# Two tiles at a time: the q/k/v projections of an attention pass by seven block products instead of eight

## The chip, the cores and the metric

The kernel runs on one core of a Trainium2 chip, all in float32. A core has five engines, each with its own queue of instructions that it works through in order: TensorE (PE in the profile, its weight loads PEld), VectorE (DVE), ScalarE (ACT), GpSimd (POOL) and SyncE (SP), which here only issues DMA transfers; ScalarE and GpSimd issue some too. An engine waits for another through semaphores. The metric is device time of one execution in microseconds (us), median of several runs.

## The reference

The input x is 4 x 1024 rows of 1024 numbers, so 4096 rows. Three blocks are added to it in turn: half of a gated feed-forward block, an attention block, and half of the feed-forward block again with the same weights.

```python
x = x + 0.5 * ffn(layernorm(x))     # dense = xn @ W.T + bias, masked
x = x + attn(layernorm(x))          # q, k, v, scores over (d, e) per row and head
x = x + 0.5 * ffn(layernorm(x))

# ffn
dots = softmax(xn @ centroids.T / 0.1);  hits = dots > 0.01
query_sel = any(hits, axis=1);           row_sel = any(hits, axis=0)[assignments]
out = where(query_sel[:, None] & row_sel[None, :], xn @ W.T + bias, 0)

# attn: 32 heads of 32, k and v have 8 heads, each used by 4 q heads
scores = einsum('bsde,..': q[d, h] * k[e, h], summed over h) / sqrt(32)
out = softmax(scores) @ v
```

The attention mixes no rows: for each row it makes a 32 x 32 matrix of scores from that row's own q and k, summed over the heads. Since k and v repeat over four heads, q is summed over those four first, and q, k and v together are 768 columns.

## The kernel before

A *tile* is 128 rows; there are 32. The kernel makes three passes over them. The order of instructions on every engine is the order of the Python code (a manual schedule); there is no planner. Helpers written as generators are advanced by `next`, so that parts of them fall between other work.

**First pass.** For each tile: layernorm, transposition, the last 256 columns of `xn @ W.T` with the 64 cluster logits (`ffn_part`, L194, L199), and the gate (`gate`, `gate_exp`, `gated`, L297 to L321). The other 768 columns are done for two tiles at once (`winograd`, L235, matmuls L253): four blocks of the two tiles by four blocks of the weights in seven block products of 4 matmuls (128 x 384) instead of eight. `token_sums` (L220, L229 to L232) makes four sums of token blocks on GpSimd, `weight_sums` (L208, L217) four sums of weight blocks, once. Meanwhile `weights` (L469) loads the projection weights into `wqkv` and, once, the cluster assignment into a one-hot matrix `hot` (L523, L524). The transposed W lies in `wc` in SBUF through all passes.

**Second pass**, the loop `for s in range(NT + 5)` (L781). It is a pipeline over tiles; in step s:

- tile s+2: layernorm statistics on VectorE (`moments`, L156, L158, root L159 on ScalarE) and the normalised row (`normed`, L174);
- tile s+1: transposition on TensorE (tp, L184), copied out by ScalarE (L185);
- tile s: the projection to q, k, v (`project`, L637): 2 halves of 8 matmuls each of 128 x 384 (L191), each half evicted by VectorE with its bias (L644). Between the halves stands `between()` (L810): the masking of tile s+3 on VectorE (L350), after which GpSimd adds it to x (L361), and the normalised row of tile s-3. The result goes to DRAM and comes back with heads across partitions (`rearranged`, L651);
- tile s-1: keys spread out on GpSimd (`keys`, kd, L667), values transposed (L678);
- tile s-2: scores (`scores`, sc, L687: small matmuls, then max and difference on VectorE L696, L698), Exp on ScalarE (L790), transposition and sums (`weighted`, L707 to L719), then the product with v (`attend`, po, L728), which VectorE reads in four instructions into `o` (L738, L740);
- tile s-3: attention added to x on GpSimd (L753, L757);
- tile s-4: transposition of the second layernorm; tile s-5: the last 256 columns and logits of the third block (ff, L191), its gate, and DMA of the tile's state to DRAM by GpSimd (L773, L774, L796).

So TensorE's order in a step is sc, tp, projection, po, tp, ff. Scores and po use PSUM in turn, in a single buffer of four banks:

```python
ps = psum2.tile([P, 4, 2, 256], F32, tag="att", name=f"sc{t}")
po = psum2.tile([P, 4, 2, 256], F32, tag="att", name=f"po{t}")
```

The next of the two therefore waits until VectorE has read the one before. All other products share four banks ("mm"). Rows of 1024 numbers live in one pool of 26 buffers ("row"); a buffer is given out again when its last reader is done, DMA stores among them.

**Third pass.** The remaining 768 columns of the third block with `winograd`, from W in `wc`.

Of the kernel before, what the change touches and what calls it, by code (L numbers as in the profile page):

```python
# [33 lines left out]
KEPT = 6  # L34
WARM = 16
# [4 lines left out]
def kernel(  # L40
# [14 lines left out]
):  # L55

# [119 lines left out]

    def transposed(xn, name):
# [30 lines left out]
    def weight_sums(ts, bstep, engine):  # L208


        w11, w12 = wc[:, :4, :HALF], wc[:, :4, HALF : 2 * HALF]
        w21, w22 = wc[:, 4:, :HALF], wc[:, 4:, HALF : 2 * HALF]
        t1, t2, t3, t4 = ts
        sub = ALU.subtract
        engine.tensor_tensor(bstep, brow[:, HALF : 2 * HALF], brow[:, :HALF], sub)
        for o, p, q in ((t1, w12, w11), (t2, w22, t1), (t3, w22, w12), (t4, w21, t2)):
            engine.tensor_tensor(o, p, q, sub)  # L217
            yield

    def token_sums(a, b, name):  # L220
# [101 lines left out]


    hot = const.tile([NCL, EMB], F32, name="hot")
# [13 lines left out]
    def row_mask(csel_b, which):  # L338
# [29 lines left out]
    with (  # L368
# [100 lines left out]
        def weights(step):  # L469
# [49 lines left out]
            elif step == 2 * KT + 1:  # L519
                asg = data.tile([P, EMB], I32, tag="row", bufs=ROWS, name="asg")[:NCL]  # L520
                nc.sync.dma_start(out=asg, in_=assign.partition_broadcast(NCL))
                yield
                nc.vector.tensor_copy(hot, asg)  # L523
                nc.vector.tensor_scalar(hot, hot, cidx, None, ALU.is_equal)  # L524

        pending = iter(())
        sc, sb, ss, es = {}, {}, {}, {}

# [16 lines left out]
        for t in range(3):  # L545
# [6 lines left out]
            if t == 0:  # L552
                for c in (5, 0, 1, 2):
                    columns(c)
                ss[0] = token_sums(0, 1, 1)
            if t == 1:
                for _ in weight_sums(*ts, nc.gpsimd):
                    pass
# [5 lines left out]
        for t in range(3, NT):  # L564
# [29 lines left out]
            if t % 2 == 1:  # L594
                ss[t - 1] = token_sums(t - 1, t, 1)
# [11 lines left out]
        ss[a] = token_sums(a, a + 1, 1)  # L607
# [6 lines left out]
        mask = row_mask(clusters, 0)  # L614
# [17 lines left out]
    with (  # L632
# [4 lines left out]
        def project(src, t, between):  # L637

            sb = attn.tile([P, NQKV], F32, tag="qkv", name=f"qkv{t}")
# [9 lines left out]
            return flat  # L649

# [52 lines left out]
        def weighted(s, t):  # L703
# [5 lines left out]
            )  # L709
            sm = small.tile([P, 2, 4, 4], F32, tag="asm", name=f"asm{t}")  # L710
# [49 lines left out]

        xn3, flat, qkv, kd, st, rs, ot = {}, {}, {}, {}, {}, {}, {}
        e = None
# [8 lines left out]
        def store_2(a):  # L771
# [5 lines left out]
        ts = (  # L777
            [wqkv[:, 4 * i : 4 * i + 4, h * HALF : (h + 1) * HALF] for i in (0, 1) for h in (0, 1)],
            bqkv[:, :HALF],
        )  # L780
        for s in range(NT + 5):  # L781
            b, g, f, a = s - 2, s - 3, s - 4, s - 5
            if has(s + 4):
                load_2(s + 4)
            if has(b):
                sc = scores(qkv[b][0], kd.pop(b), b)
            if has(s + 1):
                xT2[s + 1] = transposed(xn2.pop(s + 1), f"2_{s + 1}")
            if has(b):
                nc.scalar.activation(sc, sc, AF.Exp, scale=QK_SCALE)  # L790
            if has(s - 1):
# [5 lines left out]
            if has(a - 1):  # L797
                gated(e, a - 1, 1)
                if a - 1 < FIRST_KEPT:
                    store_2(a - 1)  # L800
            if has(s + 2):
                mv = moments(xt[s + 2], f"2_{s + 2}")
            if has(b):
                st, rs[b] = weighted(sc, b)
            if has(s + 2):
                xn2[s + 2] = normed(xt[s + 2], mv, f"2_{s + 2}")
# [9 lines left out]
            if has(s):  # L816
                flat[s] = project(xT2.pop(s), s, between)
            else:
                between()
                k = s - NT  # L820
                if k < 2:
                    rest(s - 6)
                    if k == 0:
                        sums = weight_sums(*ts, nc.vector)
# [4 lines left out]
                if 2 <= k < 4:  # L829
# [4 lines left out]
                    for _ in range(6 - k):  # L834
                        next(steps)
            if has(b):
                fo = attend(st, qkv.pop(b)[1], b)
            if has(s):
# [5 lines left out]
            if has(f):  # L844
                xT[f] = transposed(xn3.pop(f), f"3_{f}")
            if 1 <= s <= 4:

                next(held[(s - 1) // 2])
# [123 lines left out]
```

## Time and profile before

| | |
|---|---|
| median of 3 runs | 1370.59 us (1369.7 to 1370.83) |
| profiled execution, its own time | 1369.98 us |
| its span (first to last instruction) | 1368.3 us |
| mean granted TensorE clock | 0.995 of full |
| busy: TensorE / VectorE / GpSimd / ScalarE | 1346.3 / 896.2 / 475.8 / 455.1 us |
| second pass, roughly | 458 to 1082 us of the span |

In rows of a timeline the first number is the start in the span, the second the time covered, then engine, line, operation, `out<-in`, shape and number of records; in brackets the idle time before and who ended it. A row of windows gives a stretch and its length, busy time and instruction count of TensorE, weight loads, VectorE, ScalarE and GpSimd, then the granted TensorE clock, the DMA share and GB/s. Float32 matmuls of 128 x 384 appear as two records each. Each row of groups gives line, engine, operation, names, shapes, count, busy time, mean in ns, and the idle time before.

### The profile page before, as it was taken

To read this page: it belongs to the slowest core of one execution; us is meant where nothing else is said; L and a number is where in the kernel's file an instruction comes from. 1 tells how busy PE (TensorE), PEld (TensorE's weight loads), DVE (VectorE), ACT (ScalarE), POOL (GpSimd) and SP (SyncE) were. 2 spreads that over 40 slices of the span, in tenths; PEclk is the share of its full clock that TensorE was granted. 3 is DMA by queue.
4 is the path that set the end of the run, shared out by engine and by line. 5 is a ranking of instruction groups with operands and counts; after the bars stand their busy time and mean duration, and the time that the engine had idled before them with its cause. 6 is when DMAs were issued, how large, how long until landed. Compare 5 with 4: busy or idle time off the path is not lost.

```text
span 1368.3 us, 22291 instructions
## 1 busy us (share of the span) xinstructions
PE 1346.3 (98%) x8590; PEld 842.9 (62%) x8590; DVE 896.2 (66%) x1803; ACT 455.1 (33%) x697; POOL 475.8 (35%) x363
## 2 busy tenths in 40 slices
PE   8899999999999999999999999999999999999998
PEld 7565656665665656666666666666666565555554
DVE  4565555554544578777778878778767547766665
ACT  4424343434320245455445455445433200000000
POOL 3511123212121234444445454445432224433330
PEclk9999999999999999999999999999999999999999
DMA  8555646585524156555555555555331227655531
GB/s 289 111 132 131 156 119 142 136 135 144 115 66 185 54 170 189 182 176 175 165 183 182 181 175 175 172 180 181 105 90 51 77 83 249 235 197 183 181 123 72
DMA packets 291466, 206.88 MB, mean 151 GB/s; under 512 B 239904, under 2 KB 250400, under 8 KB 291360
## 3 DMA queue, kind: packets, MB, share of 16 engines
q1 hardware_dynamic: 273408, 157.44, 42.4%
q0 software_dynamic: 8736, 30.68, 5.7%
q10 hardware_dynamic: 9216, 17.33, 3.3%
q8 instruction: 68, 1.11, 0.4%
q14 instruction: 38, 0.31, 0.1%
HBM read 124.37 MB, written 81.03 MB: 150 GB/s over the span
## 4 chain that ended last, share of the span: by engine, by line
PE 89%; DVE 4%; DMA 3%; ACT 1%; issue 1%; SPq 1%; POOL 0%; ACTq 0%; POOLq 0%; DVEq 0%
PE st L253 37%; PE pq L191 24%; PE ff L191 19%; PE tp L184 5%; PE sc L687 2%; PE po L728 2%; DMA x<-in_L_attn_x_dram 1%; ACT xb L399 1%; DVE bn L156 1%; DMA wn<-in_L_ffn_weight_dram 1%; DVE xT L403 1%; DVE d L350 0%; DVE wqkv L217 0%; SPq L384 0%; DMA scd<-sc 0%
## 5 line engine op out<-in xcount | busy, mean ns | idle before, releaser
L191 PE MATMUL pq<-wqkv,xT 128*128 128x384 f32 x1024 | 335.7, 486 | 0.0
L191 PE MATMUL ff<-wc,xT 128*128 128x320 f32 (+1 forms) x1088 | 309.2, 438 | 1.0 <-ACT xT L185 0.6
L191 PEld LDWEIGHTS pq<-wqkv,xT 128*128 128x128 f32 x1024 | 192.1, 190 | 127.4 <-issue 0.2
L191 PEld LDWEIGHTS ff<-wc,xT 128*128 128x128 f32 x1088 | 204.9, 191 | 89.9 <-issue 3.0
L253 PE MATMUL st<-wc,xT 128*128 128x384 f32 x496 | 170.2, 486 | 0.0
L229 POOL TENSOR_TENSOR ts<-xT 128x512 f32<-128x512 f32 x31 | 42.2, 1363 | 349.5 <-PE st L253 225.0
L253 PEld LDWEIGHTS st<-wc,xT 128*128 128x128 f32 x496 | 94.1, 190 | 63.7 <-issue 0.2
L667 POOL TENSOR_TENSOR kd<-qk,tmask 128x1024 f32<-128x1024 f32 x32 | 60.5, 1892 | 206.0 <-DMA qk<-qkvd 161.5
L156 DVE BATCH_NORM_STATS2 bn<-x 128x6 f32<-128x512 f32 x192 | 122.4, 678 | 12.9 <-POOL x L757 7.4
L253 PE MATMUL st<-ws,ts 128*128 128x384 f32 x384 | 129.5, 486 | 0.0
L159 ACT ACT_TABLE_LOAD x59 | 75.7, 1283 | 156.0 <-DVE mv L158 154.1
L174 ACT ACTIVATE xn<-x,sc 128x1024 f32<-128x1024 f32 x69 | 85.7, 1242 | 125.1 <-DVE sc L167 86.7
L361 POOL TENSOR_TENSOR x<-x,d 128x1024 f32<-128x1024 f32 x32 | 75.6, 2361 | 141.3 <-DVE sc L165 86.4
L253 PE MATMUL st<-wqkv,ts 128*128 128x384 f32 x360 | 121.2, 486 | 0.5 <-DVE d L267 0.5
L253 PEld LDWEIGHTS st<-ws,ts 128*128 128x128 f32 x384 | 72.7, 190 | 49.4 <-issue 0.8
L199 DVE TENSOR_TENSOR d<-ff,brow 128x256 f32<-128x256 f32 (+1 forms) x68 | 29.1, 428 | 110.6 <-PE ff L191 110.6
L185 ACT COPY xT<-tp 128x512 f32<-128x512 f32 x138 | 74.2, 588 | 76.3 <-PE tp L184 75.2
L253 PEld LDWEIGHTS st<-wqkv,ts 128*128 128x128 f32 x360 | 68.3, 190 | 48.3 <-DVE d L267 1.1
L253 PE MATMUL st<-wc,ts 128*128 128x384 f32 x248 | 88.6, 501 | 9.3 <-DVE d L278 9.2
L350 DVE SCALAR_TENSOR_TENSOR d<-d,qsel,mask 128x1024 f32<-128x1024 f32 (+2 forms) x68 | 91.0, 1338 | 0.7
L184 PE MATMUL tp<-ident,xn 128*128 128x128 f32 x552 | 76.1, 281 | 3.8 <-ACT xn L174 2.2
L757 POOL TENSOR_TENSOR x<-x,ot 128x1024 f32<-128x1024 f32 x32 | 75.4, 2358 | 2.5
(101 smaller groups left out, 1550.5 us busy)
## 6 DMA issues: line engine op xcount, KB each, us to landing
x<-in_L_attn_x_dram SPq DMA_DIRECT2D x64, 512.0 KB, 4.5
d<-d SPq DMA_DIRECT2D x64, 512.0 KB, 4.5
out_dram<-x ACTq DMA_DIRECT2D x30, 512.0 KB, 5.4
xb<-in_L_attn_x_dram SPq DMA_DIRECT2D x108, 128.0 KB, 4.6
y<-x POOLq DMA_DIRECT2D x26, 512.0 KB, 3.0
xTd<-xT POOLq DMA_DIRECT2D x26, 512.0 KB, 3.7
xT<-xTd SPq DMA_DIRECT2D x26, 512.0 KB, 4.7
x<-y SPq DMA_DIRECT2D x26, 512.0 KB, 5.5
```

The costliest lines, as they stand in the source:

```text
L156: nc.vector.bn_stats(st[:, i, :], src[:, i * 512 : (i + 1) * 512])
L159: nc.scalar.activation(mv[:, 1:2], mv[:, 1:2], AF.Sqrt, bias=eps)
L174: nc.scalar.activation(xn, src, AF.Identity, bias=sc[:, 1:2], scale=sc[:, 0:1])
L184: nc.tensor.transpose(tp[:, j, :], xn[:, k * P : (k + 1) * P], ident)
L185: nc.scalar.copy(t_[:, 4 * h : 4 * h + 4, :], tp)
L191: nc.tensor.matmul(p, src[:, k, :], wts[:, k, lo:hi], start=(k == 0), stop=(k == KT - 1))
L229: nc.gpsimd.tensor_tensor(s1, a21, a22, ALU.add)
L253: nc.tensor.matmul(ps, src[:, k, :], wts[:, k, :], start=(k == 0 and (held or onto is None)), stop=(k == 3), skip_group_check=onto is not ...
L350: nc.vector.scalar_tensor_tensor(d[:, sl], d[:, sl], qsel[which][:, t : t + 1], mask[:, sl], ALU.mult, ALU.mult)
L361: nc.gpsimd.tensor_tensor(xt[t], xt[t], dt_.pop(t), ALU.add)
L667: nc.gpsimd.tensor_tensor(kd, qk[:, :, D:].unsqueeze(2).to_broadcast([P, NBLK, 4, D]), tmask.unsqueeze(1).unsqueeze(3).to_broadcast([P, NB ...
L757: nc.gpsimd.tensor_tensor(xv, xv, ov, ALU.add)
```

## The change

The projections of tiles 4 to 29 are made for two tiles at once, with the same kind of seven block products as in the passes around. For that four sums of blocks of `wqkv` are needed and have no place of their own: they are written over the first 768 columns of `wc`, which the second pass does not use. These columns are stored to DRAM in the first pass (four transfers) and loaded again in steps 29 and 30. The one-hot matrix no longer has its own buffer, it is made twice in a row buffer. The statistics of the first layernorm of the second pass move from VectorE to ScalarE, which sums the row and its squares while it writes a row that is then overwritten.

```diff
+PAIRED = range(4, 30)
...
+    def sums_normed(src, name):
+        xn = row(f"xn_{name}")
+        nm = small.tile([P, 1], F32, tag="nm", name=f"nm_{name}")
+        nc.scalar.activation(xn, src, AF.Identity, scale=-1.0 / EMB, accum_out=nm)
+        sd = small.tile([P, 1], F32, tag="sd", name=f"sd_{name}")
+        nc.scalar.activation(xn, src, AF.Square, bias=nm, accum_out=sd)
+        nc.scalar.activation(sd, sd, AF.Sqrt, bias=eps, scale=1.0 / EMB)
+        yield
+        sc = small.tile([P, 2], F32, tag="sc", bufs=4, name=f"sc_{name}")
+        nc.vector.reciprocal(sc[:, 0:1], sd)
+        nc.vector.tensor_scalar(sc[:, 1:2], nm, sc[:, 0:1], None, ALU.mult)
+        nc.scalar.activation(xn, src, AF.Identity, bias=sc[:, 1:2], scale=sc[:, 0:1])
+        yield xn
...
+            elif step < 2 * KT + 5:
+                i = step - 2 * KT - 1
+                nc.sync.dma_start(out=wtd[i], in_=blocks(wc)[i])
+            elif step == 2 * KT + 6:
+                next(qsums)
+            elif step == NT - 6:
+                asg = load_assigned()
                 yield
-                nc.vector.tensor_copy(hot, asg)
-                nc.vector.tensor_scalar(hot, hot, cidx, None, ALU.is_equal)
+                hot.append(one_hot(asg))
...
+        w11, w12, w21, w22 = blocks(wc)
+        qts = w12, w11, w21, w22
+        qsums = weight_sums(wqkv, qts, [nc.gpsimd] * 3 + [nc.vector])
...
+        def project_two(a, b, ss):
+            s1, s2, s3, s4 = ss
+            t1, t2, t3, t4 = qts
...
+            u = prod(1, xT2[a][:, :4], w11)
+            add(ca[:, 0], u, b1, ALU.add)
+            yield
+            v = prod(5, s1, t1)
+            yield
+            prod(6, s2, t2, onto=u)
+            add(ca[:, 1], u, b2, ALU.add)
+            add(cb[:, 1], v, ca[:, 1], ALU.add)
+            yield
+            p = prod(2, xT2.pop(a)[:, 4:], w21)
+            add(cb[:, 0], u, b1, ALU.add)
+            add(ca[:, 0], p, ca[:, 0], ALU.add)
+            yield
+            prod(3, s4, w22, onto=v)
+            add(ca[:, 1], v, ca[:, 1], ALU.add)
+            stored(qa, a)
+            yield
+            y = prod(7, s3, t3)
+            add(cb[:, 1], y, cb[:, 1], ALU.add)
+            yield
+            prod(4, xT2.pop(b)[:, 4:], t4, onto=y)
+            add(cb[:, 0], y, cb[:, 0], ALU.add)
+            stored(qb, b)
+            yield
...
+            for i in {PAIRED.stop - 1: (0, 1), PAIRED.stop: (2, 3)}.get(s, ()):
+                nc.sync.dma_start(out=blocks(wc)[i], in_=wtd[i])
...
-            if has(s + 1):
-                xT2[s + 1] = transposed(xn2.pop(s + 1), f"2_{s + 1}")
             if has(b):
                 nc.scalar.activation(sc, sc, AF.Exp, scale=QK_SCALE)
+            if paired:
+                if not odd:
+                    two = project_two(s, s + 1, ss2)
+                next(two)
+            if has(s + 1) and s + 1 not in xT2:
+                xT2[s + 1] = transposed(xn2.pop(s + 1), f"2_{s + 1}")
...
-            if has(s):
+            if paired:
+                if odd:
+                    xT[f] = transposed(xn3.pop(f), f"3_{f}")
+                    gate_2(a)
+                else:
+                    next(two)
+                between()
+            elif has(s):
                 flat[s] = project(xT2.pop(s), s, between)
...
+            if odd and s + 1 in PAIRED:
+                xT2[s + 2] = transposed(xn2.pop(s + 2), f"2_{s + 2}")
+                ss2 = token_sums(xT2, s + 1, s + 2, "2q")
...
+            for _ in range({1: 1, 4: 2}.get(s, 0)):
+                next(qsums)
...
+            if paired:
+                if odd and s < PAIRED.stop - 1:
+                    gate_2(f)
+            elif has(a) and a not in es:
+                gate_2(a)
```

TensorE's order in a pair becomes, in the even step: sc, products 1, 5, 6, 2 and 3, po, transposes of tile s-4; in the odd step: sc, product 7, transposes of tile s+1, product 4, transposes of tile s-4, logits of tile s-5, po, transposes of tile s+2, logits of tile s-4. Each of the three further calls of `next(two)` in the even step stands between VectorE's instructions of the attention, so the adds fall among them; the last one there (product 3 and its add) comes directly ahead of `between()`. The logits of two tiles are thus made in the odd step, together with both gates.

## The prediction

> **What bounds the kernel now.** I read the page first (shares by engine, the chain that ended last, the groups of instructions), then the timeline of single engines in one step of the second pass, then the windows around the few places where TensorE stood still.
>
> ```profile
> PE 1346.3 (98%) x8590; PEld 842.9 (62%) x8590; DVE 896.2 (66%) x1803; ACT 455.1 (33%) x697; POOL 475.8 (35%) x363
> ...
> PE 89%; DVE 4%; DMA 3%; ACT 1%; issue 1%; SPq 1%; POOL 0%; ACTq 0%; POOLq 0%; DVEq 0%
> ...
> L191 PE MATMUL pq<-wqkv,xT 128*128 128x384 f32 x1024 | 335.7, 486 | 0.0
> ```
>
> TensorE sets the time: 98% busy, 89% of the chain. The projections (pq) are 335.7 us, and TensorE never stood idle before one. A float32 matmul is two records, so 1024 records are 512 matmuls. How a step is packed is seen in TensorE's timeline (start, duration):
>
> ```profile
> 717.94 1.07 PE L687 MATMUL sc<-kd,qk 32*32 32x128 f32 x64
> ...
> 719.87 10.49 PE L191 MATMUL pq<-wqkv,xT 128*128 128x384 f32 x32
> 730.29 1.07 PE L728 MATMUL po<-stt,vt 32*32 32x128 f32 x64
> 731.28 1.09 PE L184 MATMUL tp<-ident,xn 128*128 128x128 f32 x8
> 732.21 4.47 PE L191 MATMUL ff<-wc,xT 128*128 128x320 f32 x16
> 736.62 1.07 PE L687 MATMUL sc<-kd,qk 32*32 32x128 f32 x64
> ```
>
> From start to start: scores 1.00 (the transposes follow at 718.94), transposes 0.93, projection 10.42, attend (po) 0.99, transposes 0.93, logits (ff) 4.41: 18.68 us a step, no gap. Between po and the next sc lie 5.34 us of other work. That matters because sc and po take turns in one PSUM buffer ("att", one copy of four banks): sc may start only when VectorE has read po into o. VectorE in the same step:
>
> ```profile
> 728.07 0.51 DVE L644 TENSOR_TENSOR qkv<-pq,bqkv 128x384 f32<-128x384 f32 x1
> 728.50 1.27 DVE L350 SCALAR_TENSOR_TENSOR d<-d,qsel,mask 128x1024 f32<-128x1024 f32 x1
> 729.69 0.15 DVE L165 RECIPROCAL sc<-mv 128x1 f32<-128x1 f32 x1
> 729.88 0.21 DVE L167 TENSOR_SCALAR sc<-mv,sc 128x1 f32<-128x1 f32 x1
> 730.39 0.56 DVE L644 TENSOR_TENSOR qkv<-pq,bqkv 128x384 f32<-128x384 f32 x1 [0.30 <-PE pq L191]
> 731.39 0.48 DVE L738 TENSOR_SCALAR o<-po,tmask 128x256 f32<-128x256 f32 x1 [0.44 <-PE po L728]
> 731.91 1.52 DVE L740 SCALAR_TENSOR_TENSOR o<-po,tmask,o 128x256 f32<-128x256 f32 x3
> ```
>
> The masking (L350) runs during the second half of the projection, so o starts 1.10 us after po starts and ends 3.2 us before sc wants the buffer.
>
> **The change, part by part.** *Matmuls.* A pair of tiles needs 7 products of 4 matmuls, 28 instead of 32. One costs 10.42 / 16 = 0.651 us, so a pair saves 2.61 us and 13 pairs 33.9 us, all on the chain: packed, a pair falls from 37.37 to 34.76 us.
>
> *VectorE.* 8 adds of 128x384 instead of 4 (0.48 us each from start to start): +1.9 us a pair. Statistics of one layernorm go, 1.43 us a tile (two L156, one L158: 722.08 to 723.51): -2.9. In sum it gets lighter (it idled 3.7 of 18.68 us), so its total is no bound; its order is the question, below.
>
> *ScalarE.* Two more passes over a tile; nearest row 1.24 us (L174), plus 0.19 to read an accumulator (L309): +2.9 on the 9.3 us of a step. 12.2 of 17.4: hidden. The bounds are 2.1 (a 1024-wide Exp takes 1.06 each) and 2.9; I take 2.9. It lengthens the way to the normalised row. In the odd step (pair's start as zero, its sc at 14.02+4.40 = 18.4, both below): VectorE's two reads of sc to 22.0, Exp to 23.1, copies 1.1, two passes 2.9, table 1.28, root 0.29, scale 0.4, last pass 1.24: ready at 30.3, wanted by the transposes at 18.42+1.0+2.61+0.93+2.61+0.93+4.41+0.99 = 31.9.
>
> *GpSimd.* Token sums, 1.36+1.35+1.33+1.60 = 5.6 us a pair on 18.0 (two of each row of L667, L753, L757, L361 and three issues): 23.6 of 34.8. The transposes end at 32.8, ScalarE's other pass and the copies at 35.9, the first sum at 37.3, so about when the next pair starts; it is needed 3.6 us later (sc, product 1), and the others have more time. Hidden; without that cover each would cost up to 1.4.
>
> *W.T out and back, the assignment twice.* Four stores in the first pass, four loads of 0.8 MB issued on SP's queue in steps 29 and 30 and first used in step 32, two steps of some 18 us later; a 0.5 MB load lands in 4.5 us. The second one-hot (0.68+0.74 us on VectorE) falls where VectorE waited 4.6 us for logits. Zero; if the loads were late, some 5 us once.
>
> *The moved wait.* In the even step the logits no longer lie between po and sc: TensorE's new order is product 3, po, transposes, sc of the next step. And `between()` (masking, scales) now stands behind the add that waits for product 3. With po's start as zero (it is 1.00 + 5x2.605 = 14.02 us into the pair): that add starts at 0.10 (730.39 against 730.29) and takes 0.48; masking 1.19; reciprocal and scale 0.20+0.14: o starts at 2.11. From o's start to sc's start this trace has one case where o was late, in the drain of the pass:
>
> ```profile
> 1050.62 0.48 DVE L738 TENSOR_SCALAR o<-po,tmask 128x256 f32<-128x256 f32 x1
> 1051.13 1.52 DVE L740 SCALAR_TENSOR_TENSOR o<-po,tmask,o 128x256 f32<-128x256 f32 x3
> ...
> 1052.91 1.06 PE L687 MATMUL sc<-kd,qk 32*32 32x128 f32 x64 [0.40 <-DVE o L740]
> ```
>
> 2.29 us. So sc starts at 4.40, and TensorE was free at 0.99+0.93 = 1.92: a **wait of 2.48 us in every pair**, 32.2 us in all. Behind sc on TensorE stands everything; the gain is taken back within 0.13 us a pair. Bounds: 1.5 if o started straight behind po (1.10+2.29-1.92), 3.0 if masking meets contention. I take 2.48, since the order is fixed and each term is a row. In the odd step the next tight place is the add between the two halves of product 7: 0.10+0.56+0.26 = 0.92 under transposes of 0.93; o there ends 1.4 us before it is needed.
>
> *Ends.* In step 4 the third T sum on GpSimd (3.44 us, row L217) comes behind an x+d add that waits for the masking: done 1.86+2.36+3.44 = 7.7 after po's start, needed at 5.4: about 2.5 us once. In step 30 sc follows po directly, and VectorE evicts the logits first (0.11+1.0), then scales (0.34), then o (2.29): 3.74-0.99 = 2.75 us once.
>
> *The clock.* Here a rule and a row disagree, and it decides the sign. The Trainium skill, TensorE: Matmul & The Clock Gate, in its section on what is actually happening, has the clock halved only after a whole idle window of about 3.4 us; by that a 2.5 us wait costs itself alone. This trace, where TensorE waited 1.54 us and then transposed:
>
> ```profile
> 1082.68 1.32 PE L184 MATMUL tp<-ident,xn 128*128 128x128 f32 x8 [1.54 <-DVE d L264]
> 1083.99 6.26 PE L191 MATMUL ff<-wc,xT 128*128 128x320 f32 x16
> ...
> 1083.00:1084.00 1.00, 1.00 (x9) 0.53 (x6) 0.87 (x3) 0.96 (x2) 0.00 (x0) 1.00 0.02 8
> 1084.00:1085.00 1.00, 1.00 (x3) 0.63 (x3) 1.00 (x3) 0.94 (x2) 0.00 (x0) 0.62 0.00 0
> 1085.00:1086.00 1.00, 1.00 (x3) 0.67 (x2) 0.47 (x1) 0.92 (x1) 0.00 (x0) 0.50 0.00 0
> ```
>
> (in the windows the third number from the right is the granted clock). It fell to 0.50, and the logits took 6.26 us instead of 4.47: 1.8 us. Waits of 0.99 (three) and 1.46 us between full matmuls did not do it; one of 4.61 us made the next product 5.42 instead of 2.74 (2.7 us). The page's Part 4 adds that transposes do not count as work in the same way. In the new pair, po, transposes, wait and sc make 5.4 us without one full matmul. So I expect the drop in most pairs. Bounds 0 and 2.7; nearest row 1.8, less what of the slow stretch falls into the wait and what pairs escape: 1.4, times 13 = 18.2, and 2.4 for the two ends.
>
> Sum on the profiled execution's span: 1368.3 - 33.9 + 32.2 + 2.5 + 2.75 + 18.2 + 2.4 = 1392.5; 1.7 lie around the span (1369.98 - 1368.3), and the median is 0.6 above that run: about 1395. I say **1394**.
>
> **Rivals.** *The wait without the clock* (rule right, row an accident): 1392.5 - 18.2 - 2.4 + 2.3 = 1374. For it: attend and scores are matmuls too, and may keep the clock. Against: the row. *The wait is short*, the other side: o comes directly behind po, 1.5 us a pair, clock kept: 13x1.47 = 19.1, and 1368.3-33.9+19.1+5.25+2.3 = 1361. The point from which it decides: with full clock a wait of 2.2 us a pair is even with before (28.6 of 33.9-5.25). Against it: masking stands ahead of o in VectorE's order. *A second chain comes late*: the Trainium skill, SBUF — State Buffer, section on the two separate sides, calls the port pair of VectorE and GpSimd an exclusive lock for operations with two SBUF inputs. In this trace the `best` update (L321) takes 0.27 to 2.31 us. In the odd step two such updates meet the keys (1.89 us) and x+ot (2.36 us) ahead of the transpose that po needs. By the undisturbed row the odd step has 1.3 us to spare and loses nothing; by the lock VectorE comes 2.3 us later and loses about 1: 13 more, 1407. *The change does not do what it says*: excluded; 28 matmuls a pair stand in the order.
>
> **How the numbers follow.** Wait and clock drop 0.55 (1384 to 1402); with a second late chain 0.17 (1400 to 1420); wait alone 0.15 (1369 to 1379); short wait 0.13 (1340 to 1370). Within 0.2% is 1367.9 to 1373.3, about what this measurement can tell. Of the wait alone 0.10 lies above that and 0.05 in it, of the short wait 0.01 in it and 0.12 below: slower 0.55+0.17+0.10 = 0.82, same 0.06, faster 0.12. The range leaves a tenth at each end: 1367 to 1409; the likeliest case alone 1384 to 1402.
>
> **What would show it.** sc waiting for o (VectorE, last of four) some 13 times, near 2.5 us each; a granted clock below 1 in the second pass, product 7 longer than 2.6 us; the pair near 38.6 us from score to score; GpSimd and ScalarE not named by TensorE. Wrong if the clock row stays at 1.0 there (then 1374), or if no wait on o is seen (then near 1340 to 1361).

## The result: slower by 0.8%, about half of what was forecast

The changed kernel takes 1381.54 us (median of 4 runs, 1379.09 to 1385.51) against 1370.57: ratio 1.0084, 95% interval 1.0059 to 1.0109. The forecast was 1394, in a range of 1367 to 1409. The sign was right, and so was the wait that was forecast; how often that wait brings TensorE's clock down was not: 11 us more instead of 23.

The profiled execution took 1379.09 us, its span is 1377.4 at a mean granted clock of 0.987. The page's busy times, the chain and the new projections:

```profile
PE 1324.7 (96%) x8486; PEld 831.5 (60%) x8486; DVE 897.4 (65%) x1768; ACT 518.7 (38%) x817; POOL 550.7 (40%) x418
...
PE 87%; DVE 6%; POOL 2%; ACT 2%; issue 1%; DMA 1%; ACTq 0%; SPq 0%; DVEq 0%
...
L713 PE MATMUL qs<-wc,ts_2q 128*128 128x384 f32 x312 | 113.2, 515 | 1.8 <-POOL wc L236 1.8
```

TensorE has 104 records less: 52 matmuls, four in each of 13 pairs. Its busy time fell by 21.6 us (1346.3 to 1324.7) while the span grew by 9.1, so it now stands still 31 us longer. The view of TensorE's waits (us in total, times, longest) names where:

```profile
PE sc L789 <- POOL x L393: 29.9, 13, 2.3
...
PE sc L789 <- DVE o L843: 2.8, 2, 2.4
PE qs L713 <- POOL wc L236: 1.8, 1, 1.8
```

The scores wait 13 times, once in each pair, 2.30 us each. The releaser named is GpSimd's x+d, where the forecast had said VectorE's o. That name is inferred from the last event; the timelines of one pair (TensorE, then VectorE and GpSimd) show how near the two are:

```profile
722.72 1.07 PE L831 MATMUL po<-stt,vt 32*32 32x128 f32 x64
723.72 1.09 PE L202 MATMUL tp<-ident,xn 128*128 128x128 f32 x8
727.11 1.51 PE L789 MATMUL sc<-kd,qk 32*32 32x128 f32 x64 [2.30 <-POOL x L393]
728.55 5.28 PE L713 MATMUL qs<-wc,ts_2q 128*128 128x384 f32 x8
```

```profile
722.83 0.56 DVE L742 TENSOR_TENSOR qkv<-qs,qkv 128x384 f32<-128x384 f32 x1 [0.59 <-PE qs L713]
723.30 1.27 DVE L382 SCALAR_TENSOR_TENSOR d<-d,qsel,mask 128x1024 f32<-128x1024 f32 x1
...
724.82 0.48 DVE L841 TENSOR_SCALAR o<-po,tmask 128x256 f32<-128x256 f32 x1
725.33 1.52 DVE L843 SCALAR_TENSOR_TENSOR o<-po,tmask,o 128x256 f32<-128x256 f32 x3
...
724.67 2.34 POOL L393 TENSOR_TENSOR x<-x,d 128x1024 f32<-128x1024 f32 x1 [6.58 <-DVE sc L168]
```

po starts, the add of product 3 (L742) and the masking (L382) run ahead of o, o ends at 726.85, the scores start at 727.11. GpSimd's x+d ends at 727.01, just as near, but the scores need none of its result; the first experiment separates the two. In this pair a second thing is seen: the product behind the scores takes 5.28 us instead of 2.7. TensorE ran at half clock there; such a drop of the granted clock to 0.50 is called a fall from here on. In windows of 3.41 us (busy time and instructions of TensorE, weight loads, VectorE, ScalarE, GpSimd, then the granted clock), this pair and one that stayed at full clock:

```profile
723.29:726.70 3.41, 1.52 (x40) 1.08 (x34) 3.27 (x8) 1.71 (x3) 2.03 (x1) 0.99 0.29 115
726.70:730.11 3.41, 3.00 (x67) 1.92 (x68) 1.92 (x4) 1.77 (x2) 0.31 (x1) 0.50 0.62 115
730.11:733.52 3.41, 3.41 (x7) 1.80 (x6) 1.03 (x1) 1.06 (x1) 1.51 (x1) 0.50 0.58 128
733.52:736.93 3.41, 3.41 (x17) 2.32 (x16) 3.02 (x5) 2.59 (x5) 3.33 (x3) 1.00 0.72 264
```

```profile
839.27:842.68 3.41, 1.70 (x56) 1.25 (x39) 3.27 (x8) 1.54 (x2) 1.86 (x1) 1.00 0.30 118
842.68:846.09 3.41, 2.83 (x70) 1.94 (x71) 2.38 (x4) 1.94 (x3) 0.49 (x1) 1.00 0.55 101
```

The wait is the same 2.30 us in both. In the first pair a window with 1.52 us of work is followed by two at half clock; in the second, one with 1.70 us by none. Only 5 of the 13 pairs fall (and step 30). From one even step's scores to the next, a pair without a fall takes 37.25 to 37.27 us (the last one, which has fewer logits and transposes behind it, 34.44); the four later pairs with a fall take 38.50, 40.15, 38.74 and 38.54, so 1.24 to 2.89 us more. The first pair takes 41.34: 1.8 for the late weight sum and about 2.3 for its fall. The wait costs a pair 37.26 - 34.76 = 2.50 us, a little more than the 2.30 of its record. The sum for the span:

| term | forecast | measured |
|---|---|---|
| 13 x 4 matmuls saved | -33.9 | -33.9 (52 matmuls at 0.651) |
| wait for o in 13 pairs | +32.2 | +32.5 (13 x 2.50) |
| third T sum, once | +2.5 | +1.8 |
| step 30, wait for o | +2.75 | +2.4 |
| half clock in the pairs | +18.2 | +9.2 |
| half clock at the two ends | +2.4 | +1.5 (step 30 alone; the first pair's fall is in the row above) |
| end of the pass and third pass | - | -3.8 |
| rest | - | -0.6 |
| change of the span | +24.2 | +9.1 |

From the last scores (1052.91 us before, 1065.87 now) to the end of the span it is 315.4 us before and 311.5 now. The wait of 1.54 us at 1082.68, from which the forecast took its row for the clock, and the fall behind it are missing in the changed kernel's trace. The same transposes there follow their predecessor without idle time:

```profile
1093.93 1.19 PE L202 MATMUL tp<-ident,xn 128*128 128x128 f32 x8
```

That wait hangs, through VectorE and GpSimd, on the attention's result coming back from DRAM, for which GpSimd waited 3.32 us before and 1.49 now. Of the twelve experiments below only the one with full matmuls in the wait shows it again (1.43 us, without a fall). What brings the transfer sooner isn't shown.

The other three runs of the changed kernel had mean clocks of 0.984, 0.982 and 0.982 and spans of 1378.8, 1380.9 and 1383.8 us: by their clocks they lost more to falls than the profiled one, and the median lies 2.5 us above that.

### The profile page after: what moved, and what is told of

It reads as the page before. It is cut to its first block, busy times and chain, and to the rows that moved or that the text cites. A ratio compares the mean times of both kernels' runs of the same rounds, so it can differ in the third digit from the quotient of the medians.

```text
span 1377.4 us, 22187 instructions
## 1 busy us (share of the span) xinstructions
PE 1324.7 (96%) x8486; PEld 831.5 (60%) x8486; DVE 897.4 (65%) x1768; ACT 518.7 (38%) x817; POOL 550.7 (40%) x418
## 4 chain that ended last, share of the span: by engine, by line
PE 87%; DVE 6%; POOL 2%; ACT 2%; issue 1%; DMA 1%; ACTq 0%; SPq 0%; DVEq 0%
PE st L276 37%; PE ff L209 19%; PE qs L713 18%; PE pq L209 5%; PE tp L202 4%; PE sc L789 2%; POOL x L393 2%; DVE d L382 2%; PE po L831 1%; ACT xb L431 1%; DVE bn L159 1%; DVE xT L435 1%; DMA scd<-sc 1%; PE tpw L484 0%; ACT L162 0%
## 5 line engine op out<-in xcount | busy, mean ns | idle before, releaser
L713 PE MATMUL qs<-wc,ts_2q 128*128 128x384 f32 x312 | 113.2, 515 | 1.8 <-POOL wc L236 1.8
L159 DVE BATCH_NORM_STATS2 bn<-x 128x6 f32<-128x512 f32 x132 | 84.2, 679 | 12.7 <-DMA x<-in_L_attn_x_dram 6.9
L382 DVE SCALAR_TENSOR_TENSOR d<-d,qsel,mask 128x1024 f32<-128x1024 f32 (+2 forms) x68 | 91.6, 1347 | 0.6
L713 PEld LDWEIGHTS qs<-wc,ts_2q 128*128 128x128 f32 x312 | 61.7, 202 | 46.5 <-issue 8.8
L202 PEld LDWEIGHTS tp<-ident,xn 128*128 128x128 f32 x552 | 63.3, 144 | 19.3 <-issue 10.8
L276 PEld LDWEIGHTS st<-wc,ts 128*128 128x128 f32 x248 | 47.0, 194 | 46.2 <-issue 11.5
```

The lines of the kernel that those rows point to most:

```text
L159: nc.vector.bn_stats(st[:, i, :], src[:, i * 512 : (i + 1) * 512])
L202: nc.tensor.transpose(tp[:, j, :], xn[:, k * P : (k + 1) * P], ident)
L276: nc.tensor.matmul(ps, src[:, k, :], wts[:, k, :], start=(k == 0 and (held or onto is None)), stop=(k == 3), skip_group_check=onto is not ...
L382: nc.vector.scalar_tensor_tensor(d[:, sl], d[:, sl], qsel[which][:, t : t + 1], mask[:, sl], ALU.mult, ALU.mult)
L713: nc.tensor.matmul(ps, src[:, k, :], wts[:, k, :], start=(k == 0 and onto is None), stop=(k == 3), skip_group_check=onto is not None,)
```

## The experiments

All times are medians; each group of runs has its own runs of the kernel before (1370.15, 1368.80 and 1369.44 us), so times of different groups compare to within 1 or 2 us.

**What does the wait wait for?** The masking goes behind o in the even step of a pair:

```diff
-                between()
+                if odd:
+                    between()
...
                 fo = attend(st, qkv.pop(b)[1], b)
+            if paired and not odd:
+                between()
```

> The changed kernel with one move: in the even step of a pair the masking and the scales of the other layernorm stand behind o on VectorE instead of ahead of it. Theory (VectorE's o holds sc up): o starts 1.0 us earlier, so the wait ahead of the odd step's scores falls from 2.30 to about 1.3 us in each of 13 pairs (-13 us), and with a shorter wait the clock drops less often (-9 us if never): 1358 to 1369 us. Rival (the x+d addition on GpSimd, which the profile names as the one that ended the wait, holds it up): the masking and so x+d come about 2 us later, the wait grows to about 4.3 us, 1405 us or more.

1364.51 us (1363.74 to 1367.33), ratio 0.9961 [0.9946, 0.9975]. TensorE's timeline and waits:

```profile
720.44 1.07 PE L831 MATMUL po<-stt,vt 32*32 32x128 f32 x64
721.43 1.09 PE L202 MATMUL tp<-ident,xn 128*128 128x128 f32 x8
723.84 1.06 PE L789 MATMUL sc<-kd,qk 32*32 32x128 f32 x64 [1.32 <-DVE o L843]
```

```profile
PE sc L789 <- DVE o L843: 20.0, 15, 2.4
...
PE qs L713 <- POOL wc L236: 7.3, 1, 7.3
```

VectorE and GpSimd in the same pair:

```profile
722.06 1.52 DVE L843 SCALAR_TENSOR_TENSOR o<-po,tmask,o 128x256 f32<-128x256 f32 x3
...
724.87 2.35 POOL L393 TENSOR_TENSOR x<-x,d 128x1024 f32<-128x1024 f32 x1 [9.07 <-DVE sc L168]
```

The wait shrank to 1.32 us and bears o's name. GpSimd's x+d now starts after the scores have started, so they don't wait for it; it holds nothing up but the first pair: there the third weight sum, behind it on GpSimd, comes 7.3 us late. The later pairs take 36.34 to 36.36 us, and none falls. So the order of masking and o on VectorE is the difference between a loss and a gain of this change: 17 us, which is about 13 x 0.98 = 12.7 less wait and some 9 less clock, with 5.5 more for the weight sum.

**What is the clock worth?** Four full matmuls that nobody reads fill the wait:

```diff
+            if paired and odd:
+                fill = bank(f"fill{s}")[:, :HALF]
+                for k in range(4):
+                    nc.tensor.matmul(
+                        fill, ident, wqkv[:, k, :HALF], start=(k == 0), stop=(k == 3)
+                    )
```

> The changed kernel with four more matmuls of 128 x 384 in each odd step, between the transposes and the scores, whose result nobody reads: they stand where TensorE waits. Theory (the clock falls because of the wait): no wait on o is left, no drop of the clock in the second pass, 2.61 us of filler in place of 2.30 us of waiting: 1379 - 9 + 4 = 1374 us, and the runs agree within 1 us instead of 6. Rival (the slow stretches have another cause, such as the pairs' denser products): slow stretches stay, 1383 us or more.

1375.49 us (1372.76 to 1376.71), ratio 1.0039 [1.0026, 1.0052]. The time is as expected; the runs still spread over 4 us, where 1 was expected. Every pair behind the first takes 37.48 or 37.49 us, none falls; the one fall left is at step 30. The filled pairs are themselves 0.22 us longer, 0.2% in all, so that the wait, paid in full and without the falls, would have made this change slower by about 0.2%. In the changed kernel the falls add some 6 to 9 us.

**What counts as standing still?** The same place filled with 20 unread transposes, so that TensorE is never idle but does no full matmul:

```diff
+            if paired and odd:
+                fill = bank(f"fill{s}").rearrange("p (j c) -> p j c", j=4)
+                for j in range(20):
+                    src = wqkv[:, j % 4, :P]
+                    nc.tensor.transpose(fill[:, j % 4, :], src, ident)
```

> The changed kernel with 20 unread transposes of 128x128 (0.116 us each, 2.3 us) on TensorE in the place of the wait for o, in the odd step of every pair: TensorE is never idle there, but does no full-sized matmul. If transposes don't count as work for the clock: falls stay as they were, about 5 of 13 pairs, about 1380 us. If they count (it is the idle time alone that brings the clock down): no fall in the pairs, and 1371 to 1376 us, as with full matmuls in that place.

1372.25 us (1370.13 to 1374.32), ratio 1.0027 [1.0020, 1.0034].

```profile
720.74 1.07 PE L831 MATMUL po<-stt,vt 32*32 32x128 f32 x64
721.74 1.09 PE L202 MATMUL tp<-ident,xn 128*128 128x128 f32 x8
722.67 2.35 PE L906 MATMUL fill<-ident,wqkv 128*128 128x128 f32 x20
725.13 1.06 PE L789 MATMUL sc<-kd,qk 32*32 32x128 f32 x64
```

Here 5.4 us pass without one full matmul, and no pair falls; all but the first take 37.25 to 37.29 us. So these transposes count as work for the clock. Whether they count as much as full matmuls isn't shown: at half weight they would leave some 1.2 us of standing still, and no trace here shows a fall at that. Either way it takes away the argument by which the forecast put the fall into most pairs.

**Does a longer wait fall more often?** Two unread `bn_stats` on VectorE between the scales and o:

```diff
+                if not odd:
+                    again = small.tile([P, 2, 6], F32, tag="again", name=f"again{s}")
+                    for i in range(2):
+                        nc.vector.bn_stats(again[:, i, :], xt[g][:, i * 512 : (i + 1) * 512])
```

> The changed kernel with two unread bn_stats of 512 elements on VectorE between the scales and o in the even step of every pair; nothing else differs. From the trace of the changed kernel one costs about 0.6 us, so o and with it the scores of the odd step come about 1.3 us later: the wait on o goes from 2.3 to about 3.6 us, 13 x 1.3 = 17 us. Theory (the clock falls when a stretch without full-sized matmuls is long enough, and 2.3 us of waiting is just at the edge, so that only 5 of 13 pairs fall): now 11 or more of the 13 fall, at 1.2 to 2.9 us each; 1405 to 1415 us. Rival (whether a pair falls is chance and doesn't hang on the length of the wait): about 5 of 13 fall again, 1397 us.

1418.06 us (1413.96 to 1419.00), slower, ratio 1.0348 [1.0324, 1.0372].

```profile
738.95:742.36 3.41, 1.12 (x14) 0.86 (x8) 3.30 (x8) 2.12 (x3) 2.35 (x1) 1.00 0.28 115
742.36:745.77 3.41, 2.22 (x65) 1.47 (x66) 1.92 (x4) 1.36 (x2) 0.00 (x0) 0.50 0.40 68
745.77:749.18 3.41, 3.41 (x7) 1.87 (x6) 1.78 (x2) 1.06 (x1) 0.80 (x1) 0.50 0.57 106
```

All 13 pairs fall, each for about 6.8 us. The theory holds, but the price of a fall was set too low: the pairs behind the first take 40.95 to 41.12 us, 1.3 of the 3.7 above 37.26 is wait and 2.4 clock. The falls begin at 537.6, 578.5, 619.5, 660.5 and so on, 41.0 us apart.

That even spacing led to a look at all traces, here with those of the runs below included. Within each of the 14 (before, after and the twelve experiments) the falls begin on one grid of 3.413 us, to within 0.1 us. In the changed kernel they begin at 535.5, 576.5, 726.7, 767.6, 880.3 and 1010.0; the distances divided by 3.413 are 12.0, 44.0, 12.0, 33.0 and 38.0. Between 140 and 1330 us they last one or two cells of it; what decides between one and two stays open. I then added up, from the gaps in TensorE's records in that stretch, how long it stood still in each cell of the grid at full clock, and whether the next cell was at half clock:

| standing still in a cell of 3.41 us | followed by half clock | not |
|---|---|---|
| under 1.5 us | 0 | all the rest |
| 1.5 to 1.9 us | 8 | 24 |
| over 1.9 us | 44 | 0 |

The two limits are read off these same traces, no run was made to test them, and with the grid known to 0.1 us they are no sharper than that. The row that made the forecast (1.54 us of waiting ahead of a transpose at 1082.68 in the kernel before) is the lowest of the eight. A wait of 2.30 us at a random place of the grid puts over 1.9 us into one cell with a chance of (1.51 + 0.40)/3.41 = 56%. In the profiled run it was 5 of 13, since the places are not random: a pair of 37.26 us is 10.92 cells, so that the wait slides by 0.3 us from pair to pair, and each fall pushes it on. In the changed kernel the cells ahead of a fall hold 1.85 us or more of standing still, and in no pair without a fall does a cell hold more than 1.75.

**Is there a sharp threshold?** One unread full matmul in the wait's place, which leaves 1.65 us:

```diff
+            if paired and odd:
+                fill = bank(f"fill{s}")[:, :HALF]
+                nc.tensor.matmul(fill, ident, wqkv[:, 0, :HALF], start=True, stop=True)
```

> The changed kernel with one unread matmul of 128x384 (0.65 us) in the place of the wait for o, in the odd step of every pair; the scores start when they did before, so that the edit itself saves and costs nothing. Theory formed from the runs so far: the clock is judged in fixed windows of 3.41 us that stand on one grid through a whole run, and is halved for the next window where TensorE stood still for more than some 1.77 us of one. The matmul leaves 1.65 us of standing still in a pair, below that in whatever place the grid lies: no fall in the 13 pairs (one where the weight sum comes late and one at step 30 may stay), 1371 to 1377 us. Rival (a fall is chance, the more likely the longer the wait): 1.65 of 2.30 us leaves 3 or 4 of the 13 pairs falling, 1377 to 1381 us.

1376.81 us (1372.43 to 1378.66), at the upper edge of the theory's range, and its threshold does not hold: besides the first pair (2.28 us for the late weight sum) two pairs fall, fewer than the 3 or 4 of the rival. Two cells of this run, the second figure being TensorE's busy time; the first was followed by half clock, the other wasn't:

```profile
687.70:691.11 3.41, 1.76 (x67) 1.02 (x66) 2.30 (x6) 3.36 (x4) 2.06 (x1) 0.99 0.25 63
691.11:694.53 3.42, 3.42 (x6) 1.75 (x6) 2.29 (x2) 1.18 (x2) 0.27 (x1) 0.51 0.94 166
```

```profile
875.40:878.80 3.40, 1.75 (x68) 0.94 (x66) 2.41 (x6) 3.06 (x4) 2.35 (x1) 1.00 0.26 81
878.80:882.20 3.40, 3.40 (x22) 2.25 (x16) 2.93 (x4) 1.16 (x2) 0.00 (x0) 1.00 0.74 135
```

The wait lies whole in one cell eleven times, and two of the eleven fall. So chance at this length isn't excluded; what tells these cells from the others between 1.5 and 1.9 us stays open.

**Logits between attend and scores again**, one tile in each step:

```diff
-                    gate_2(a)
...
-            if paired:
-                if odd and s < PAIRED.stop - 1:
-                    gate_2(f)
-            elif has(a) and a not in es:
+            if has(a) and a not in es:
                 gate_2(a)
-            for i in sorted(es) if odd or not paired else ():
-                es[i] = gate_exp(es[i], i, 1)
+            for i in sorted(es):
+                if not isinstance(es[i], tuple):
+                    es[i] = gate_exp(es[i], i, 1)
```

> The changed kernel with the logits of one tile in each step, behind the attend product and its transposes, as before the change, instead of two tiles in the odd step. Theory: the wait for o goes (4.4 us of logits cover it), but in the odd step nothing of length is left ahead of the transposes of tile s+2, so these wait about 2.8 us for the normalised row that ScalarE makes: about 1375 us, the wait has only moved. Rival (ScalarE's statistics cost nothing wherever they stand): no wait there, 1342 us.

1394.90 us (1390.90 to 1400.87), ratio 1.0184 [1.0148, 1.0219]: worse than the change itself, and 20 us above what I expected. The wait for o is gone from all pairs but the first; in its place stand

```profile
PE tp L202 <- ACT xn L192: 30.4, 12, 2.7
...
PE po L831 <- DVE stt L809: 5.5, 9, 0.8
```

The logits of tile s-5 no longer stand ahead of po in the odd step, po and the transposes of tile s+2 follow 4.4 us earlier, and the normalised row from ScalarE isn't ready. The size of that wait was expected; the clock, which falls in 6 pairs besides the first, and the wait of po were not. The change had two waits of nearly the same size in store, and moving the logits of one tile traded one for the other.

**The statistics on VectorE again**, the rest of the change kept (`moments` and `normed` in place of `sums_normed`):

```diff
-                normal = sums_normed(xt[s + 2], f"2_{s + 2}")
-                next(normal)
+                mv2 = moments(xt[s + 2], f"2_{s + 2}")
...
-                xn2[s + 2] = next(normal)
+                xn2[s + 2] = normed(xt[s + 2], mv2, f"2_{s + 2}")
```

> The changed kernel with the statistics of that layernorm on VectorE again, all the rest of the change kept. Theory (the statistics lie off TensorE's path, in slack of ScalarE and VectorE alike): no different from the changed kernel, 1376 to 1386 us. Rival (the change lives from the lighter VectorE): 1.4 us more in front of VectorE's work for each tile, o or the reads of sc come later, 1390 us or more.

1386.99 us (1384.15 to 1389.70). I expected no difference; the median is some 5 us more. The intervals of the two ratios overlap (1.0096 to 1.0144 here, 1.0059 to 1.0109 for the changed kernel), but the pairs show it too: VectorE's busy time is 935.8 us instead of 897.4, the pairs that don't fall take 37.73 us and more instead of 37.26, and two more pairs fall in the profiled run. So the move to ScalarE is worth a little; neither theory had it. That it helps by lightening VectorE ahead of o is likely, but not shown.

**A full matmul group in the wait's place.** Product 7 (four matmuls; the expectations call it the first half, since product 4 is summed onto it) needs nothing that comes late. It goes ahead of the odd step's scores:

```diff
-                next(two)
+                    next(two)
...
             if has(f) and f in xn3:
                 xT[f] = transposed(xn3.pop(f), f"3_{f}")
+            if paired and not odd:
+                next(two)
```

> The changed kernel with the first half of product 7 moved from behind the odd step's scores to ahead of them, into the place where TensorE waits; no work is added. Theory: the wait falls from 2.30 to about 0, no clock drop there; the odd step's transposes of tile s+2 come 2.6 us earlier and now wait about 1 us for the normalised row: 1340 us without that wait, 1353 with it. Rival (the gain of the block products is lost to something other than this wait): 1370 us or more.

1355.96 us (1355.93 to 1356.52), ratio 0.9897 [0.9882, 0.9911]. In this version product 7 of tiles 4 and 5 comes ahead of the third weight sum and is made without it. No wait for o is left in the pairs, but they take 35.89 to 36.09 us where packed ones would take 34.76: TensorE waits in small pieces for ScalarE (`tp<-ACT xT`, 3.5 us in 11 waits, so only part of the 1.1 us a pair), and 3.2 us for the weight sum in the first pair.

With the two sums made at the end of step 3 instead of 4:

```diff
-            for _ in range({1: 1, 4: 2}.get(s, 0)):
+            for _ in range({1: 1, 3: 2}.get(s, 0)):
```

> As the run with product 7 between, with the third and fourth sums of weight blocks made at the end of step 3, so that the first pair has them before its product 7. Theory: the wait of 3.2 us for that sum in the first pair goes, and with it the fall of the clock there; the pairs stay at 36.1 us: 1350 to 1355 us. Rival (the sums collide with other work of GpSimd and VectorE in step 3): 1356 us or more.

1352.05 us (1348.71 to 1352.28), ratio 0.9862 [0.9846, 0.9878]. The first pair's wait and its fall are gone, and all tiles have their sums.

A first attempt at ScalarE's queue put statistics, root and last pass of the normalised row around the Exp, ahead of the copies:

```diff
+            if paired and odd:
+                normal = sums_normed(xt[s + 2], f"2_{s + 2}")
+                next(normal)
             if has(b):
                 nc.scalar.activation(sc, sc, AF.Exp, scale=QK_SCALE)
+            if paired and odd:
+                xn2[s + 2] = next(normal)
```

> A version meant to beat both: the first half of product 7 stands ahead of the scores of the odd step (so that a full matmul of 2.6 us covers the wait for o), the third and fourth sums of weight blocks are made a step earlier (so that product 7 of the first pair has them), and in the odd step the statistics and the normalised row are made before and directly behind the Exp (so that the transposes of tile s+1 don't wait for the row, the 0.3 us and more that the run with product 7 in between still showed). Theory: no wait left in the pair, 34.8 to 35.4 us from pair to pair, 1336 to 1348 us. Rival (the chain through VectorE and ScalarE, and the SBUF port that VectorE and GpSimd share, now set the end): 35.8 us or more a pair, 1352 us or more.

1375.90 us (1375.68 to 1377.71): the rival's case, 24 us more than without this edit; two pairs fall, and one without a fall takes 37.55 to 38.06 us. TensorE's waits, ScalarE's timeline, and VectorE's last work ahead of the Exp:

```profile
PE tp L202 <- ACT xT L203: 18.5, 13, 1.4
PE ff L209 <- DVE qkv L749: 14.1, 12, 1.5
```

```profile
725.70 0.29 ACT L187 ACTIVATE sd<-sd,eps 128x1 f32<-128x1 f32 x1
726.01 1.28 ACT L908 ACT_TABLE_LOAD   x1
727.30 1.06 ACT L908 ACTIVATE s<-s 128x1024 f32<-128x1024 f32 x1
728.26 1.23 ACT L192 ACTIVATE xn<-x,sc 128x1024 f32<-128x1024 f32 x1
729.40 1.05 ACT L203 COPY xT<-tp 128x512 f32<-128x512 f32 x2
...
725.84 1.23 DVE L800 TENSOR_TENSOR s<-sc,amx 128x1024 f32<-128x1024 f32 x1
```

The root ahead of the Exp needs another function table, and loading the Exp's takes 1.28 us. That holds the Exp up only a little: its input is ready at 727.07, it starts at 727.30. The last pass, 1.2 us, then stands in the way of the copies that TensorE waits for. Where the second wait (for VectorE's add of product 4) comes from isn't shown.

The second attempt leaves only the two passes ahead of the Exp, where ScalarE had idled 2.5 us, puts root and last pass behind the copies, and copies tile s-4 out ahead of the second layernorm's root:

```diff
         nc.scalar.activation(xn, src, AF.Square, bias=nm, accum_out=sd)
+        yield
         nc.scalar.activation(sd, sd, AF.Sqrt, bias=eps, scale=1.0 / EMB)
         yield
...
+            if paired and odd:
+                normal = sums_normed(xt[s + 2], f"2_{s + 2}")
+                next(normal)
             if has(b):
                 nc.scalar.activation(sc, sc, AF.Exp, scale=QK_SCALE)
...
+                def last_product():
+                    if paired and odd:
+                        next(two)
+                        xn2[s + 2] = next(normal)
...
+            if paired and odd:
+                xT[f] = transposed(xn3.pop(f), f"3_{f}")
             if has(g):
                 mv = moments(xt[g], f"3_{g}")
```

> As product7_sums_step3, and in the odd step the two statistics passes stand ahead of the Exp on ScalarE, root and last pass follow the copies of tile s+1 directly, VectorE's two scale instructions stand behind the eviction of product 7, and tile s-4 is copied out ahead of the root of the second layernorm. Theory (what the pair still lost, 1.3 us, was TensorE waiting for ScalarE, whose queue ran the passes behind the Exp): 34.8 to 35.4 us a pair, 1335 to 1345 us. Rival (the passes wait for the row of tile s+2 from GpSimd and hold up the Exp behind them): 36 us a pair or more, 1352 us or more.

1343.64 us (1342.91 to 1345.16), ratio 0.9808 [0.9793, 0.9822]: 26 us below the kernel before.

```profile
708.25 1.07 PE L832 MATMUL po<-stt,vt 32*32 32x128 f32 x64
709.25 1.09 PE L203 MATMUL tp<-ident,xn 128*128 128x128 f32 x8
710.18 2.75 PE L714 MATMUL qs<-wc,ts_2q 128*128 128x384 f32 x8
712.85 1.07 PE L790 MATMUL sc<-kd,qk 32*32 32x128 f32 x64
```

Product 7 covers the wait; a pair takes 35.22 to 35.23 us, 0.46 above the packed one, and no pair falls. Which of the moves on ScalarE brought how much was not separated. What is left is step 30, where the scores still wait for o (3.3 us, and the clock falls behind it).

To take that away too, the logits of tiles 25 to 27 go a step earlier:

```diff
-            if paired:
-                if odd and s < PAIRED.stop - 1:
-                    gate_2(f)
-            elif has(a) and a not in es:
+            if odd and paired or PAIRED.stop <= s < NT:
+                gate_2(f)
+            elif not paired and has(a) and a not in done:
                 gate_2(a)
```

> As product7_root_late, and the logits of tiles 25 to 27 are made a step earlier, so that they stand between attend and scores in steps 29 and 30 too. Theory: the wait of 2.4 us for o in step 30 and the fall of the clock behind it go, 2 to 5 us less than product7_root_late. Rival (they come back at step 33, where now no logits lie between): no difference.

1345.33 us (1344.73 to 1346.50): nothing gained.

```profile
1024.34 1.09 PE L203 MATMUL tp<-ident,xn 128*128 128x128 f32 x8
1030.17 1.52 PE L790 MATMUL sc<-kd,qk 32*32 32x128 f32 x64 [4.74 <-DVE o L844]
```

The wait comes back, longer, where the logits are now missing, with a fall of 6.8 us behind it. That was the rival.

## Why the prediction was right in its sign and wrong in its size

*The matmuls.* Right: 52 fewer, 33.9 us.

*The moved wait.* Right, term by term. o starts 2.10 us after po (724.82 against 722.72; forecast 2.11), the scores 2.29 after o (forecast 2.29), and a pair without a fall takes 37.25 us (forecast 37.24, from 34.76 + 2.48). The wait's record reads 2.30 instead of 2.48 because the record of the transposes ends 0.17 us later than the packed distance that I had counted. The sign "GpSimd not named" failed, since the profile names GpSimd; that the scores wait for o was shown by moving the masking.

*VectorE, ScalarE, GpSimd, DMA.* In the changed kernel none of them sets a further wait in the pairs. One of VectorE's `best` updates took 2.32 us beside GpSimd's x+ot, as the rival of the second chain had it, but the wait did not follow: the price was right, the slack was larger than I allowed. Costing the statistics' move at nothing was not quite right: moved back they cost some 5 us.

*Ends.* 1.8 and 2.4 us instead of 2.5 and 2.75, and 1.5 us for the fall at step 30. What lies behind the second pass was put at nothing and came out at -3.8 us, as a wait and its fall are missing there: no step of the forecast led to that.

*The clock: the step that failed.* "So I expect the drop in most pairs", and with it 1.4 x 13 = 18.2 us, which is a fall of 1.8 us in ten of them. In the profiled run 5 of 13 pairs fell, at 1.24 to 2.89 us, 9.2 in all. The price of one fall was near (1.8 from the row; 9.2 / 5 = 1.8 measured); its frequency was wrong. Two arguments led there. The first was that transposes don't count as work in the same way, which the Trainium skill has in TensorE: Matmul & The Clock Gate, Part 4. The run of 20 transposes speaks against it: they kept the clock at full through 5.4 us without a full matmul. Whether they would also raise it, which is what the page speaks of, no run here shows. The second was to take one row with a fall after 1.54 us for the rule; of the cells with 1.5 to 1.9 us of standing still only 8 of 32 were followed by a fall. The page's other rule, in its section on what is actually happening, that the clock falls after a whole idle window of about 3.4 us, is not borne out either: in these traces over 1.9 us within one window always brought a fall, and a wait of 2.3 us is not safe. What the same section says of the window itself, 3413 ns and free-running, is what the traces show (3.413 us, one grid through the run, in another place in each trace), and I had left it out: with it the question would have been how much of the wait falls into one cell. By the table's row over 1.9 us that is an estimate of 56%, 7 of 13 pairs at 1.8 us, 13 us instead of 18.2, and 1392.5 - 5.2 = 1387 for the span. The four spans were 1377.4 to 1383.8; of the profiled one's distance 3.8 us are the missing wait behind the second pass.

*The rivals.* The wait without the clock was costed at 1374 and is what the two fills measure (1375.49 and 1372.25). The result lies between it and the likeliest case, since some pairs fall and others don't: I had treated as one or the other what happens pair by pair. The sign did not hang on the falls, as I had thought: without them the change is still 0.2 to 0.3% slower. The short wait, with masking behind o, was costed at 1361 and measured 1364.51; the late weight sum of the first pair, which I had not moved along with the masking, is 7.3 us there against 2.5 in my sum, more than the whole difference.

## What to carry to other kernels

When a product between two users of one buffer is taken out, ask what else can stand there before counting the gain: here product 7, which needs nothing late, turned +0.8% into -1.4% with the sums a step earlier, and -1.9% with ScalarE's queue put in order. In these traces a wait on a busy TensorE was priced by its length and by its place against the clock's windows: with under 1.5 us of standing still in one window it cost only itself; between 1.5 and 1.9 us it brought a fall in 8 of 32 cases, with over 1.9 us always, at some 1.2 to 2.9 us each. Filling the gap for 2.3 us with matmuls or transposes that nobody reads avoided the falls. A releaser named by the profile can be the last event and not the dependence; where two engines end within 0.2 us, move the work of one of them and look again.

## What the runs showed of the hardware that I had not expected

- The half clock comes in whole cells of a grid of 3.413 us that stays fixed through an execution and lies elsewhere in the next trace; all 52 falls between 140 and 1330 us in the 14 traces lie on it.
- With a wait of 3.5 us in each pair the pair settled at 40.95 to 41.12 us, 12 cells of the grid (40.96): the falls and the wait locked to each other, so that every pair paid. That the lock is more than a coincidence of lengths was not tested.
- Transposes kept the clock up where full matmuls did (20 of them in 2.35 us: no fall in 13 pairs).
- A change of function table on ScalarE took 1.28 us each time, but even directly ahead of the Exp it delayed it by only 0.2 us, because VectorE was still making the Exp's input.
